# A graph layer on one core: table rows of two blocks and two relations by seven products of halves, weight sums on VectorE, and a table stage laid out by the list scheduler

## The chip, the cores and the metric

The kernel runs on one core of a Trainium2 chip. Its time is the device time of one execution in microseconds (us), from the records of the runs. TensorE (PE) multiplies matrices into PSUM, VectorE (DVE) and ScalarE (ACT) do elementwise work, GpSimd (POOL) does small elementwise work and issues the gathers from DRAM, and SyncE (SP) issues the plain transfers.

## The reference

One layer of a relational graph network on 625 nodes with 512 features. 20,625 edges (10,000 in both directions and one loop a node), sorted by target, have a source, a target, one of four relations and a weight. All is f32.

```python
h = maximum(layernorm(x), 0)
xs = h[src]
msg = sum over r of (xs @ W_rel[r] + b_rel[r]) * where(edge_type == r, edge_weight, 0)[:, None]
agg = segment_sum(msg, dst) / maximum(segment_sum(edge_weight, dst), 1)
t  = h @ W_self + b_self + agg
x1 = layer_norm(h + t, ln1_g, ln1_b)
ffn = gelu(x1 @ W_ffn1 + b_ffn1) @ W_ffn2 + b_ffn2
out = x + layer_norm(x1 + ffn, ln2_g, ln2_b)
```

W_rel is four matrices of 512 x 512, W_self one, W_ffn1 is 512 x 1024 and W_ffn2 1024 x 512.

## The kernel before

The nodes lie in five blocks of 125 rows (128 partitions are used). Two stages follow each other, and the second is in part begun inside the first.

**Table stage.** `h @ W_rel[r]` is worked out once for every node and relation. Each of the 20 pieces (`table_rows(r, i)`, relation r, block i) is one PSUM bank of 128 x 512 that four f32 matmuls fill, one for each 128 of the 512 inner features (the page counts two records for an f32 matmul, line L390). ScalarE empties the bank (L398), multiplying by the block's reciprocal standard deviation, for the normalization leaves that factor out: `pre_norm` (L352) only subtracts the mean and takes the maximum with zero. The row then goes to a DRAM table (L401); the last nine pieces are also kept in SBUF. The order is written out by hand: a double loop over r and i, with further work hung on chosen (r, i): the statistics and transposes of the next block, the search for the edges of each node (`find_tiles`, `rows_of_tiles`, `find_windows`, `slot_weights`, `slot_fields`), the degrees of nodes by relation, the loads of later weights (`later_loads`). Two buffers hold the four relation matrices in turn.

**Weights of the dense blocks.** For three blocks the edges are summed by matrices: for each target node, the sum of weights by (relation, source) makes a matrix `sums_w`, and the aggregate is `sums_w` times the table. It is built in 12 units (`slot_hots`: VectorE compares 16 slots with a grid and with keys, `low` L687, `eq` L690, and three products `high` L693; `slot_sums`: 16 small bf16 matmuls, L705; `empty_sums`: VectorE sums a bank, L711). Seven units (EARLY) are done inside the table stage, five behind it.

**Edge stage and rest.** The order comes from a list scheduler (`Plan`): operations have an engine, an assumed duration, dependencies and buffers that they take and give; its times settle only the order in which instructions are issued. In it: `h @ (W_self + I)` (pz, L428), the dense sums (`chunk_sum`, L1121), 82 gathers of table rows by GpSimd (L1000, L1054) that VectorE adds up seven edges at a time (L1024) for the other two blocks, with a one-hot matmul for each group (`edge_sum`; the sum is split into a high and a low part in a faster format, L1044 and L1045, apart from the last group, which is one f32 matmul, L1047), the first normalization (its root on GpSimd, L328), transposes (L335), the two layers of the feed-forward part (pu, L791, and po, L809), the second normalization and the store.

Of the kernel before, what the change touches and what calls it, by code (L numbers as in the profile page):

```python
# [68 lines left out]
class Plan:  # L69
# [6 lines left out]
    AFTER = {"PE": 1.5, "POOL": 0.8}  # L76

    def __init__(self, buffers):
        self.buffers, self.ops = dict(buffers), []

    def op(self, engine, us, fn, after=(), take=(), give=(), lag=0.08, rank=None, order=False, level=None):
        o = Plan.Op()
        o.engine, o.us, o.fn, o.take, o.give, o.lag, o.rank, o.level = engine, us, fn, list(take), list(give), lag, rank, level
        if engine == "PE":
            o.lag = max(lag, Plan.BEHIND)
        behind = Plan.AFTER.get(engine, 0.0)
        o.after = [(a, a.us if order and a.engine == engine else a.us + (0.0 if a.engine == engine == "PE" else a.lag)
                    + (behind if a.engine in ("DVE", "ACT") and a.engine != engine else 0.0)) for a in after if a is not None]
# [6 lines left out]
    def emit(self):  # L95
        for o in reversed(self.ops):
            o.tail = o.us + o.lag + max((b.tail for b in o.nexts), default=0.0)
        order = self.times()
        for o in order:
            if o.fn:  # L100
                o.fn()

    def times(self):
        left, order, t = list(self.ops), [], 0.0
        free, buffers, back = {"POOL": 3.0}, dict(self.buffers), []
# [33 lines left out]
def gnn_layer(ctx, tc, x, edges, edge_groups, firsts, fourths, windows, w_self, w_rel, w_ffn1, w_ffn2, brel_in, rows_in, bf1_in, out, n_edges):  # L139
# [38 lines left out]
    ps = ctx.enter_context(tc.tile_pool(name="ps", bufs=5, space=bass.MemoryType.PSUM))  # L178
    ps_acc = ctx.enter_context(tc.tile_pool(name="ps_acc", bufs=1, space=bass.MemoryType.PSUM))
    ps_add = ctx.enter_context(tc.tile_pool(name="ps_add", bufs=2, space=bass.MemoryType.PSUM))  # L180
# [3 lines left out]
    early = early_stack.enter_context(tc.tile_pool(name="early", bufs=1))  # L184

# [19 lines left out]
    def load_wr(r, ks=((0, KD),)):  # L205
        wr_sb.setdefault(r, None)
        if wr_sb[r] is None:
            wr_sb[r] = early.tile([P, KD, D], F32, tag="wr", name=f"wr_{r}", bufs=2)
# [18 lines left out]
    load_wr(0, [(2, 4)])  # L227
    nc.sync.dma_start(first_of_tile, bass.AP(tensor=firsts.tensor, offset=firsts.offset, ap=[[0, P], [1, NT]]))
    load_x(2, 3)
    load_x(3, NB)  # L230
    nc.sync.dma_start(ed, edges)
    load_wr(1)
# [4 lines left out]
    def later_loads(r, i):  # L237
        if (r, i) == (0, 0):
            bias_rows()
        if i == NB - 1 and r < R - 2:  # L240
            load_wr(r + 2)
        if (r, i) == (1, 2):
            nc.sync.dma_start(bf1, bf1_in)
            nc.sync.dma_start(ws_sb, w_self.rearrange("(k p) n -> p k n", p=P))
            load_rows(rows[:, :4 * D], 0, 4 * D)
            load_rows(rows[:, 5 * D:], 5 * D, 6 * D)
        if (r, i) == (2, 1):
            nc.sync.dma_start(w1_sb, w_ffn1.rearrange("(k p) f -> p k f", p=P))
        if r == 3 and i < LA:
            chunk_load(i * CH)  # L250
        if (r, i) == (2, 3):
            nc.sync.dma_start(w2_sb, w_ffn2.rearrange("(k p) n -> p k n", p=P))
# [27 lines left out]

    TB = 8
# [56 lines left out]
    def transposed(dest, in_, name):  # L338

        n = dest.shape[1]  # L340
        nc.scalar.copy(dest, turn(in_, name, n)[:, :n, :])
# [8 lines left out]
    def pre_norm(i, mean):  # L350
        if i > 0:
            nc.vector.tensor_scalar(z[:, i, :], xs[:, i, :], mean, 0.0, op0=ALU.subtract, op1=ALU.max)  # L352
# [1012 lines left out]
```

## Time and profile before

| | us |
|---|---|
| median of 3 runs (lowest to highest) | 245.45 (245.16 to 247.13) |
| the profiled execution | 246.03 |
| its span, first to last instruction | 244.0 |
| mean granted TensorE clock | 0.994 |

The span is the part of the execution that the trace shows; the remaining 2 us lie around it. In the tables of the profile, a row of a group has the line, engine, operation, tiles and shape, then "busy us, mean ns of one", then the idle time of that engine just before, with what ended it. A row of the timeline or of the chain has the start, the duration and the instruction. PEld is TensorE's loading of weights, which lies beside its matmuls.

### The profile page before, as it was taken

To read this page: it belongs to the slowest core of one execution; us is meant where nothing else is said; L and a number is where in the kernel's file an instruction comes from. 1 tells how busy PE (TensorE), PEld (TensorE's weight loads), DVE (VectorE), ACT (ScalarE), POOL (GpSimd) and SP (SyncE) were. 2 spreads that over 40 slices of the span, in tenths; PEclk is the share of its full clock that TensorE was granted. 3 is DMA by queue.
4 is the path that set the end of the run, shared out by engine and by line. 5 is a ranking of instruction groups with operands and counts; after the bars stand their busy time and mean duration, and the time that the engine had idled before them with its cause. 6 is when DMAs were issued, how large, how long until landed. Compare 5 with 4: busy or idle time off the path is not lost.

```text
span 244.0 us, 2881 instructions
## 1 busy us (share of the span) xinstructions
PE 235.2 (96%) x892; PEld 131.0 (54%) x892; DVE 190.6 (78%) x397; ACT 48.1 (20%) x87; POOL 119.1 (49%) x166
## 2 busy tenths in 40 slices
PE   7999999999999999999999999999999999999980
PEld 3454444555554555445554444457864588446860
DVE  5596399959699799999998989977987996473123
ACT  3233213212221211101020203012232042002500
POOL 6258505373100137877656788787877781110000
PEclk9999999999999999999999999999999999999997
DMA  6972586979986327677779898877966765001101
GB/s 162 357 262 61 173 267 197 371 240 358 284 275 179 125 54 210 181 205 208 198 208 334 271 305 322 297 234 247 351 201 191 210 181 163 0 1 42 45 3 46
DMA packets 20965, 48.91 MB, mean 200 GB/s; under 512 B 3162, under 2 KB 3924, under 8 KB 20818
## 3 DMA queue, kind: packets, MB, share of 16 engines
q1 hardware_dynamic: 13494, 26.11, 32.2%
q0 software_dynamic: 7152, 22.32, 30.8%
q10 hardware_dynamic: 300, 0.26, 0.4%
q8 instruction: 8, 0.13, 0.2%
q14 instruction: 11, 0.09, 0.1%
HBM read 42.27 MB, written 6.54 MB: 200 GB/s over the span
## 4 chain that ended last, share of the span: by engine, by line
PE 94%; DMA 2%; DVE 1%; SPq 1%; issue 0%
PE pt L390 28%; PE acc L1121 21%; PE po L809 14%; PE pu L791 14%; PE pz L428 7%; PE bank L705 5%; DMA wr<-in_L_gnn_W_rel_dram 2%; PE tp_x L335 1%; PE acc L1044 1%; PE acc L1045 1%; PE tp_h L335 1%; PE acc L1047 0%; PE tf L670 0%; DVE ya L828 0%; DVE y L833 0%
## 5 line engine op out<-in xcount | busy, mean ns | idle before, releaser
L1000 POOL DMA_INDIRECT ms<-table,row_i x70 | 69.8, 997 | 30.3 <-issue 12.6
L390 PE MATMUL pt<-wr,turned_x 128*128 128x512 f32 x160 | 72.1, 597 | 0.6 <-DMA wr<-in_L_gnn_W_rel_dram 0.6
L390 PEld LDWEIGHTS pt<-wr,turned_x 128*128 128x128 f32 x160 | 29.2, 190 | 32.3 <-issue 32.0
L1024 DVE SCALAR_TENSOR_TENSOR ea<-ms,wgt_g,ea 128x512 f32<-128x512 f32 x59 | 42.9, 746 | 1.3 <-DMA ms<-table,row_i 1.2
L809 PE MATMUL po<-w_sb,gelus 128*125 128x512 f32 (+2 forms) x96 | 35.5, 521 | 0.0
L791 PE MATMUL pu<-turned_x,w_sb 128*128 128x250 f32 (+1 forms) x192 | 35.3, 340 | 0.0
L791 PEld LDWEIGHTS pu<-turned_x,w_sb 128*128 128x128 f32 x192 | 31.4, 189 | 4.8 <-issue 1.9
L809 PEld LDWEIGHTS po<-w_sb,gelus 128*125 128x125 f32 x96 | 16.6, 188 | 15.3 <-issue 12.3
L398 ACT ACTIVATE m<-pt,rx 125x512 f32<-125x512 f32 x20 | 13.8, 688 | 53.4 <-PE pt L390 51.1
L711 DVE TENSOR_REDUCE sums_w<-bank 126x160 f32<-126x480 f32 x32 | 19.1, 650 | 6.2 <-PE bank L705 6.1
L705 PEld LDWEIGHTS <-low 128*128 128x128 bf16 x192 | 16.1, 147 | 13.1 <-issue 12.4
L1121 PE MATMUL acc<-tr,sums_w 126*128 126x512 f32 x44 | 20.6, 601 | 0.0
L428 PE MATMUL pz<-ws_sb,turned_x 128*128 128x512 f32 x40 | 17.8, 596 | 0.0
L1121 PE MATMUL acc<-m,sums_w 126*128 126x512 f32 x36 | 17.5, 603 | 0.0
L795 ACT ACTIVATE gelus<-pu,bf 128x250 f32<-128x250 f32 (+1 forms) x24 | 10.5, 437 | 31.5 <-PE pu L791 30.1
L705 PE MATMUL bank<-high,low 128*128 128x120 bf16 x192 | 16.2, 225 | 0.0
L693 DVE TENSOR_TENSOR high<-eq,turned 128x640 bf16<-128x640 bf16 x36 | 15.6, 487 | 0.4
L817 DVE TENSOR_TENSOR y<-po,z 125x512 f32<-125x512 f32 (+2 forms) x6 | 3.6, 602 | 14.3 <-PE po L809 14.3
L687 DVE TENSOR_TENSOR low<-turned,grid 128x2000 bf16<-128x2000 bf16 x12 | 14.3, 1192 | 0.1
L1054 POOL DMA_INDIRECT ms_first<-table,x_row x12 | 12.0, 997 | 3.5 <-issue 1.7
L1010 ACT CAST eh<-ea 128x512 fp32r<-128x512 f32 x9 | 5.3, 586 | 41.2 <-DVE ea L1024 41.2
L1121 PEld LDWEIGHTS acc<-tr,sums_w 126*128 126x128 f32 x44 | 7.9, 191 | 7.3 <-issue 6.9
(183 smaller groups left out, 241.8 us busy)
## 6 DMA issues: line engine op xcount, KB each, us to landing
tr<-table SPq DMA_DIRECT2D x10, 512.0 KB
table<-m SPq DMA_DIRECT2D x20, 224.0 KB
w_sb<-in_L_gnn_W_ffn_dram SPq DMA_DIRECT2D x2, 2048.0 KB
wr<-in_L_gnn_W_rel_dram SPq DMA_DIRECT2D x3, 1024.0 KB
xs<-in_x_dram SPq DMA_DIRECT2D x1, 1280.0 KB
ms<-table,row_i POOLq DMA_INDIRECT x70, 3.8
ws_sb<-in_L_gnn_W_self_dram SPq DMA_DIRECT2D x1, 1024.0 KB
rows<-in_rows_dram SPq DMA_DIRECT2D x1, 1024.0 KB
```

Source lines behind the costliest of these rows:

```text
L390: nc.tensor.matmul(p, hT[i][:, k, :], wr_sb[r][:, k, :], start=(k == 0), stop=(k == KD - 1))
L398: nc.scalar.activation(m[:NG], p[:NG], AF.Copy, scale=rx[:NG, i, 1:2])
L428: nc.tensor.matmul(p[0], hT[i][:, k, :], ws_sb[:, k, :], start=(k == 0), stop=(k == KD - 1))
L687: nc.vector.tensor_tensor(low[:, :, :NG, :], of[:, 0].rearrange("p (a t) -> p a t", t=TB).unsqueeze(2).to_broadcast([P, nb_, NG, TB]), gri ...
L693: nc.vector.tensor_mul(high[:, :, a * 2 * NC:(a + 1) * 2 * NC, :], eq, pairs(2 + a))
L705: nc.tensor.matmul(p[:, i * W:(i + 1) * W], low[:, t // TB, :, t % TB], high[:, t // TP, :, t % TP], start=True, stop=True)
L711: nc.vector.tensor_reduce(sums_w[OUTER[d]][:NG + 1, :, n0:n0 + 2 * QT].rearrange("p c (t h) -> p t h c", h=2), p[:NG + 1, :QT * 3 * 2 * NC ...
L791: nc.tensor.matmul(pu[:, :n_b * w], w1_sb[:, k, f * P:(f + 1) * P], turned_x[:, b0:b0 + n_b, k, :w], start=(k == 0), stop=(k == KD - 1))
L809: nc.tensor.matmul(po[h][:n, :w], gelus[:, at + i, f, :n], w2_sb[:, f, c], start=(f == 0), stop=(f == KF - 1))
L1000: nc.gpsimd.indirect_dma_start(out=ms[j], out_offset=None, in_=table[:, :], in_offset=bass.IndirectOffsetOnAxis(ap=row_i[:, j:j + 1], axis=0))
L1024: nc.vector.scalar_tensor_tensor(to, ms[j], wgt_g[:, k, q - 1:q], box["sum"], op0=ALU.mult, op1=ALU.add)
L1121: nc.tensor.matmul(acc[b,], sums_w[b][:NG + 1, c, :], kept[c][:NG + 1], start=done[b] == 1, stop=done[b] == NC)
```

## The change

**Seven products.** Blocks 1 and 2, and blocks 3 and 4, are taken in pairs (x, y); relations 0 and 1, and 2 and 3, in pairs (p, q). With the inner features in halves, a pair of blocks is a matrix of halves ((x0, x1), (y0, y1)) and a pair of relations ((p0, q0), (p1, q1)). Their product has eight half products; here it is formed from seven, with sums of the operands before and sums of results behind. Block 0 stays as it was (`plain`).

Four node sums a pair of blocks (128 x 2 x 128 elements each) and four weight sums a pair of relations (128 x 2 x 512 each) are made by VectorE. The weight sums of the second pair are written over the first pair's weights. Results are added up in PSUM: ScalarE copies a bank into the next one (`seeded`), and the following product is added to it there. Two of a unit's four rows are completed by VectorE, which adds a part that ScalarE has copied to SBUF (`row_of_two`); the other two, and block 0's, are emptied by ScalarE.

So that the sums can be formed, the normalization of blocks 1 to 4 now includes the factor (the root is needed ahead of it); for blocks 2 to 4 ScalarE does it, and the maximum with zero is in ScalarE's copy behind the transpose. Relations 2 and 3 have their weights loaded together, into the space of z and x, once all blocks are normalized and transposed; the first half of relation 1 comes ahead of block 3.

**The list scheduler** lays out the whole table stage. PSUM is five banks for products and three for the rest in this stage.

**Beside these:** five early units of slot weights in place of seven; the three products `high` of a unit are one instruction; several casts and scalings go from VectorE to ScalarE, the additions of the identity to W_self to GpSimd; the last edge group is split in two parts as the others are; some assumed durations of the second plan differ. Bank sums that the plan places behind the last product are issued in the edge stage.

```diff
-            wr_sb[r] = early.tile([P, KD, D], F32, tag="wr", name=f"wr_{r}", bufs=2)
+            wr_sb[r] = early.tile([P, KD, D], F32, name=f"wr_{r}") if r < 2 else (z, xs)[r - 2][:, :KD, :]
...
+        if i not in BY_ACT:
+            nc.vector.tensor_scalar(z[:, i, :], xs[:, i, :], mean, rx[:, i, 1:2], op0=ALU.subtract, op1=ALU.mult)
+        else:
+            nc.scalar.activation(z[:, i, :], xs[:, i, :], AF.Identity, scale=rx[:, i, 1:2], bias=rx[:, i, 2:3])
...
-    def table_rows(r, i, between=None):
...
-        nc.scalar.activation(m[:NG], p[:NG], AF.Copy, scale=rx[:NG, i, 1:2])
...
+    def row_of_two(c, p, m, e):
+        nc.vector.tensor_add(m[:NG], p[:NG], e[:NG])
...
+    def sums_of_nodes(x_, which):
+
+        S = node_sums[x_]
+        x0, x1, y0, y1 = (hT[b][:, h * HK:(h + 1) * HK, :] for b in (x_, x_ + 1) for h in range(2))
+        for n, (a, b, o) in enumerate(((y0, y1, ALU.add), (S[0], x0, ALU.subtract), (x0, y0, ALU.subtract), (x1, S[1], ALU.subtract))):
+            if n in which:
+                nc.vector.tensor_tensor(S[n], a, b, op=o)
+
+    def sums_of_weights(r, which):
+
+        T = weight_sums[r]
+        p0, p1, q0, q1 = (block_of_weights(r + n, h) for n in range(2) for h in range(2))
+        for n, (a, b) in enumerate(((q0, p0), (q1, T[0]), (q1, q0), (p1, T[1]))):
+            if n in which:
+                (nc.vector if T_ON[2 * r + n] else nc.gpsimd).tensor_tensor(T[n], a, b, op=ALU.subtract)
+
+    def product(to, of, with_, first):
+        for k in range(HK):
+            nc.tensor.matmul(to, of[:, k, :], with_[:, k, :], start=first and k == 0, stop=k == HK - 1, skip_group_check=True)
...
-        for a in range(3):
-            nc.vector.tensor_mul(high[:, :, a * 2 * NC:(a + 1) * 2 * NC, :], eq, pairs(2 + a))
-        return low, high
...
+        nc.vector.tensor_mul(high.rearrange("p n f k t -> p (n f) k t"),
+                             eq.unsqueeze(2).to_broadcast([P, np_, 3, 2 * NC, TP]).rearrange("p n f k t -> p n f (k t)"),
+                             w.rearrange("p n f t -> p (n f) t").unsqueeze(2).to_broadcast([P, 3 * np_, 2 * NC, TP]))
...
-    EARLY = 7
-    PER_ROW = 3
+    EARLY = 5
...
+                def seeded(k, of, o):
+                    return do("ACT", 0.57, lambda: nc.scalar.copy(at(k), at(of)), after=[o], take=["bank"])
+
+                o = pe(1.75, lambda: product(at("a"), x0, w(0), True), after=[turns[x_], weights if r else None], take=["bank"], read=["p0"])
+                b = seeded("b", "a", o)
+                yield
...
+                    o = pe(1.75, lambda: product(at("a"), x1, w(1), False), after=[b], read=["p1"])
+                    evicted(o, cx, names["a"], ["bank"])
...
+                o = pe(1.75, lambda: product(at("e"), node_sums[x_][0], weight_sums[r][0], True), after=[S[x_, 0], T[r, 0]], take=["bank"], read=["T0"])
+                e = do("ACT", 0.57, lambda: copied_e(names["e"]), after=[o], give=["bank"], take=["e"])
+                yield
+                o = pe(1.75, lambda: product(at("b"), node_sums[x_][1], weight_sums[r][1], False), after=[b, S[x_, 1], T[r, 1]], read=["T1"])
+                c = seeded("c", "b", o)
...
+                o = pe(1.75, lambda: product(at("b"), node_sums[x_][2], weight_sums[r][2], False), after=[c, S[x_, 2], T[r, 2]], read=["T2"])
+                d = seeded("d", "b", o)
+                f1 = evicted(o, cy + NB, names["b"], ["bank"], e=("sb_" + names["e"], e))
+                yield
+                o = pe(1.75, lambda: product(at("c"), node_sums[x_][3], w(3), False), after=[c, S[x_, 3]], read=["q1"])
+                f2 = evicted(o, cx + NB, names["c"], ["bank"], e=("sb_" + names["e"], e))
...
+                o = pe(1.75, lambda: product(at("d"), y1, weight_sums[r][3], False), after=[d, T[r, 3]], read=["T3"])
+                evicted(o, cy, names["d"], ["bank"])
...
+            here = plain(r)
+            for x_ in range(1, NB, 2):
+                there = unit(r, x_, r == 0 and x_ == 1)
+                for one in ("hhthttthtt" if r == 0 else "hhhthttttt") if x_ == 1 else "thttttt":
+                    next(here if one == "h" else there)
+                here = there
...
     def parted(unit):
-        return unit is not last_unit
+        return True
```

In the last lines "h" stands for a piece of block 0, or of the unit before, and "t" for a piece of the unit that is being formed, each of two matmuls.

More of the change, by code (lines that the diff above doesn't have):

```diff
@@ L378, in gnn_layer, with scaled_row, self_plus @@
     kept = {}
+    def scaled_row(g_bc):
+        nc.scalar.activation(g_bc, g_bc, AF.Copy, scale=1.0 / RS)
+    def self_plus():
+        for i in range(KD):
+            nc.gpsimd.tensor_add(ws_sb[:, i, i * P:(i + 1) * P], ws_sb[:, i, i * P:(i + 1) * P], ident)
     def bias_rows():
```

497 lines of the change are left out of this document (323 added, 174 removed).

## The prediction

> **What bounds the kernel now.** I read the page first (busy shares, then the chain that ended last), then the busy time by windows, then the chain of waits in order of time, and last the groups of single operations.
>
> ```profile
> PE 235.2 (96%) x892; PEld 131.0 (54%) x892; DVE 190.6 (78%) x397; ACT 48.1 (20%) x87; POOL 119.1 (49%) x166
> PE 94%; DMA 2%; DVE 1%; SPq 1%; issue 0%
> 0.00:85.80 85.80, 83.81 (x318) 41.61 (x319) 65.61 (x180) 20.23 (x34) 30.52 (x75) 1.00 0.73 235
> 85.80:161.70 75.90, 75.90 (x262) 37.17 (x260) 71.53 (x121) 9.68 (x16) 53.64 (x55) 1.00 0.75 236
> 161.70:210.50 48.80, 48.80 (x191) 34.70 (x190) 38.76 (x66) 12.90 (x25) 32.01 (x34) 1.00 0.67 205
> ```
>
> The window rows give length, then PE, PEld, DVE, ACT and POOL busy. The table stage runs from 0 to 85.8 us; behind it PE has no idle time at all up to 210.5. VectorE is 76% busy in the table stage (65.61 of 85.80), 94% in the first part of the edge stage (71.53 of 75.90), 79% after it. So TensorE is the bound, VectorE is close behind it, and the question is whether TensorE work that goes away is replaced by waiting for VectorE.
>
> **The products.** Twenty table rows of four f32 matmuls each were 80 matmuls. Now block 0 keeps four per relation (16), and each of four units (two blocks by two relations) has seven products of two matmuls (56): 72. Eight matmuls go, and each is two records (160 records for 80).
>
> ```profile
> L390 PE MATMUL pt<-wr,turned_x 128*128 128x512 f32 x160 | 72.1, 597 | 0.6 <-DMA wr<-in_L_gnn_W_rel_dram 0.6
> 20.89 18.89 PE pt L390 x44
> L705 PE MATMUL bank<-high,low 128*128 128x120 bf16 x192 | 16.2, 225 | 0.0
> 203.89 0.57 PE L1044 MATMUL acc<-eh,oh 128*128 128x512 f32 x1
> 204.31 0.39 PE L1045 MATMUL acc<-el,oh 128*128 128x512 f32 x1
> 204.54 3.54 PE L791 MATMUL pu<-turned_x,w_sb 128*128 128x250 f32 x16
> 209.63 1.02 PE L1047 MATMUL acc<-es,oh 128*128 128x512 f32 x2
> 210.48 8.75 PE L809 MATMUL po<-w_sb,gelus 128*125 128x512 f32 x20
> ```
>
> The mean of 597 ns holds overlap; the undisturbed stretch gives the step: 18.89/44 = 0.429 us a record. 16 x 0.429 = **6.9 us off PE**. The last group of edges is now split in a high and a low part as the others are: 0.65 us (203.89 to 204.54) in place of 0.85 (209.63 to 210.48), **0.2 us off PE**. Two of seven early units of slot weights move from the table stage behind it; that moves 32 of the 192 bank matmuls, 2.7 us, and saves nothing. Warm-up, transposes and bytes of weights are as many as before. With no new wait the profiled execution, 246.03 us for its span of 244.0, would become 246.03 - 7.1 = 238.9. The median of the runs shown, 245.45, lies 0.6 below that execution, so on its scale the floor is 238.3.
>
> **What VectorE is given.**
>
> ```profile
> L500 DVE TENSOR_TENSOR found<-ends,node_f 128x810 f32<-128x810 f32 x1 | 1.0, 1003 | 0.0
> L537 DVE TENSOR_TENSOR found<-ends,node_f 128x192 f32<-128x192 f32 x1 | 0.4, 357 | 0.0
> L817 DVE TENSOR_TENSOR y<-po,z 125x512 f32<-125x512 f32 x4 | 2.8, 691 | 5.2 <-PE po L809 5.2
> L687 DVE TENSOR_TENSOR low<-turned,grid 128x2000 bf16<-128x2000 bf16 x12 | 14.3, 1192 | 0.1
> L693 DVE TENSOR_TENSOR high<-eq,turned 128x640 bf16<-128x640 bf16 x36 | 15.6, 487 | 0.4
> L711 DVE TENSOR_REDUCE sums_w<-bank 126x160 f32<-126x480 f32 x32 | 19.1, 650 | 6.2 <-PE bank L705 6.1
> L352 DVE TENSOR_SCALAR z<-xs,mv_x 128x512 f32<-128x512 f32 x4 | 2.2, 543 | 0.1
> L952 DVE TENSOR_TENSOR ws_sb<-ws_sb,ident 128x128 f32<-128x128 f32 x4 | 1.1, 281 | 0.0
> L955 DVE TENSOR_SCALAR rows<-rows 128x512 f32<-128x512 f32 x2 | 0.8, 419 | 0.0
> L558 DVE CAST fields<-slot_f 128x384 bf16<-128x384 f32 x1 | 0.4, 424 | 0.0
> ```
>
> No sum of weights stands in the trace. Its size is 1024 f32 elements; the two "found" rows give (1003 - 357)/618 = 1.045 ns an element, so 1.23 us, and the bounds are 1.00 (the 810 row) and 2.0 (the 810 row taken twice). Eight are 9.8 us. Eight sums of nodes (256 elements) at 0.42 are 3.4. Eight rows are now finished by a VectorE addition from PSUM, 8 x 0.69 (the L817 row) = 5.5. Added: 18.7. Taken out: two early units, each 1.19 + 4 x 0.49 + 4 x 0.65 = 5.7, together 11.5 (moved, not saved); three normalizations, four additions on the self weights, two scalings (1.6 + 1.1 + 0.8) and nine casts, at most 0.42 each and mostly half as large, which I take as 2.5: 6.0, to ScalarE and GpSimd. The three multiplications of a unit become one of 1920 elements; the bf16 rows of 640 and 2000 elements give 0.49 + 1280 x 0.52 ns = 1.15 against 3 x 0.49, 0.3 a unit. If the new form loses the rate of those rows it costs 1920 x 1.045 ns = 2.0, 0.5 more a unit; I take the gain, since the operands have the same inner pairs as now.
>
> Table stage: 65.6 + 18.7 - 11.5 - 6.0 - 5 x 0.3 = 65.3 us of VectorE in 85.8 - 6.9 - 2.7 = 76.2 us, 86%. That is under the 94% at which PE has no idle time in the trace. Behind it: 71.5 + 38.8 + 11.5 - 7 x 0.3 + 0.7 (the extra low part) = 120.4 in 124.7 + 2.7 - 0.2 = 127.2 us, 95% in place of 88%. This is the tight place: if all of the moved work falls in the first part, that holds some 81 us in 78.6, so about 3 us must slide into the part that is 79% busy. I take 0.8 us of PE idle there, bounds 0 and 5.
>
> **The round trips.** In a unit ScalarE copies a partial sum from one PSUM bank to another and TensorE adds to the copy: twelve such seeds and four copies to SBUF.
>
> ```profile
> L341 ACT COPY turned_x<-tp_h 128x512 f32<-128x512 f32 x4 | 2.3, 586 | 7.1 <-PE tp_h L335 7.1
> 9.07 1.92 PE L390 MATMUL pt<-wr,turned_x 128*128 128x512 f32 x4
> 11.10 0.69 ACT L398 ACTIVATE m<-pt,rx 125x512 f32<-125x512 f32 x1 [1.24 <-PE pt L390]
> ```
>
> ScalarE starts 0.1 us after the modelled end of its matmuls (9.07 + 1.92 = 10.99, then 11.10). So a seed takes 0.1 + 0.59 + about as much back, near 0.8 us. In the order of the pieces each seed has one other product between it and its use, four records, 1.7 us. It is covered with 0.9 us to spare; if that cover goes, it costs 0.8 each. ScalarE, 20.2 us busy in 85.8, gets 16 copies (9.4), three normalizations and the casts and gives eight evictions back: under half full. A seed queued behind another ScalarE copy can still be late now and then: 0.5 us in all, bounds 0 and 10 (twelve times 0.8). The node and weight sums are VectorE's, and PE, in order, holds every later product and slot sum behind one that waits for them; a row finished by VectorE holds one of the five banks that the next unit needs. Within the 86% I leave that in the same 0.5.
>
> **The first microseconds.** The load order changes (first half of relation 1 ahead of block 3), and normalizing now needs the reciprocal root from GpSimd first.
>
> ```profile
> 7.70 1.10 PE L390 MATMUL pt<-wr,turned_x 128*128 128x512 f32 x2 [0.59 <-DMA wr<-in_L_gnn_W_rel_dram]
> 10.41 0.69 DVE L369 BATCH_NORM_STATS2 st_x<-xs 128x6 f32<-128x512 f32 x1 [1.98 <-DMA xs<-in_x_dram]
> 142.22 0.75 DVE L1024 SCALAR_TENSOR_TENSOR ea<-ms,wgt_g,ea 128x512 f32<-128x512 f32 x1
> 142.49 0.60 POOL L328 TENSOR_TENSOR rs_z<-rs_z,half 128x1 f32<-128x1 f32 x1
> 149.32 0.74 DVE L752 SCALAR_TENSOR_TENSOR za<-z,mv_z,rows 128x512 f32<-128x512 f32 x1
> 149.58 0.89 POOL L328 TENSOR_TENSOR rs_z<-rs_z,half 128x1 f32<-128x1 f32 x1
> ```
>
> Block 2 lands at 10.41. Statistics 0.69, three small VectorE steps (an estimate of 0.5), root 0.6, normalization 0.69, transposes 0.44, ScalarE's copy 0.59, node sum 0.42, and eight hand-overs at an estimated 0.2 end near 15.9. PE, from 7.70, has 0.86 of the first product left, four half rows at 1.72 and two sets of transposes until it wants that sum: 16.3. So 0.4 us in hand, and any delay lands on PE: 0.8 us, bounds 0 and 3. The weights of relations 2 and 3 are now loaded together into the space of x and z; they are wanted after some nineteen pieces, past 40 us, and I charge nothing, or up to 2 us if that cover goes.
>
> Beside VectorE work that reads one SBUF operand (142.22) the root takes 0.60 us; beside work that reads two (149.32) it takes 0.89. The sums of weights read two and are longer. [...]
>
> **Is the gather chain a floor?**
>
> ```profile
> 89.25 1.15 POOL L1000 DMA_INDIRECT ms<-table,row_i  x1 [6.63 <-PE pz L428]
> 200.71 1.51 POOL L1000 DMA_INDIRECT ms<-table,row_i  x1 [0.30 <-issue]
> 204.74 0.75 DVE L1024 SCALAR_TENSOR_TENSOR es<-ms,wgt_g,ea 128x512 f32<-128x512 f32 x1
> 219.07 0.60 PE L335 MATMUL tp_x<-ident,x 128*128 128x128 f32 x4
> ```
>
> GpSimd gathers table rows from 89.25, 3.4 us behind the table, to 202.2; the last row is added at 205.5. The matmul of that group waits in PE's order until 209.63, and the last transposes until 219.07: 13.6 us behind the last row, for about 6 us of dependent work. So some 7 us of room, and the chain itself starts up to 9.6 us earlier. Even if VectorE stretches it by 5, it does not end last.
>
> **Sum.** 246.03 - 6.9 - 0.2 + 0.8 + 0.5 + 0.8 = 241.0; on the scale of the median **240.4 us**.
>
> **The rivals.** *The full root-and-sum collision* at the start: GpSimd's root held for the length of a weight sum (1.2 us) in blocks 1 and 2, 2.4 us in place of part of my 0.8: 242.5. For it: the 0.89 us row and only 0.4 us in hand. Against: at that time most weights for the sums have not landed. Chance 0.08. *VectorE becomes the bound* in the edge stage: at no more than 94% its 81 us need 86 where PE needs 78.6, and half of that difference is made good later: 4 us, 244.5 (243 to 247). For it: 94% already. Against: room after 161.7 and in the table stage. Chance 0.15. *Seeds on the path*, the slower case: ScalarE's copy, in ScalarE's queue behind evictions and field copies, comes after PE has run out of the one covering product. Each then costs 0.8 plus a queued eviction's 0.69, 1.5 x 12 = 18 in all less the cover that remains, a third: 12 us, so 250.3. It decides against the change from 7.1/12 = 0.6 us a seed. For it: every product of a unit hangs on another engine, where the trace has none such. Against: ScalarE's free time. Chance 0.11. *No effect*, PE idle exactly where products went, 245.5: chance 0.02.
>
> **How the numbers follow.** The forecast has 0.64, by itself 238.2 to 242.3. One per cent (about what a measurement tells from no change) is 243.0 and 247.9. Faster: 0.64 + 0.06 + 0.02 (the low end of VectorE's bound) = 0.72; within: 0.02 + 0.11 + 0.02 = 0.15; slower: 0.11 + 0.02 = 0.13. The range 238.2 to 245.8 leaves out the seeds (0.11), the top of VectorE's bound (0.04) and 0.05 below.
>
> **What would show it.** Right: 144 table records with steps of 0.43, table stage over near 77 to 79, PE idle of 2 to 3 us more than before. Wrong: PE waiting on ScalarE copies inside units (seeds), on node sums before 20 us (root), or gaps in PE between 85 and 160 that end on slot weights (VectorE); and weight sums well over 1.3 us, or the merged product near 2.

## The result: 3242 us, because the plan lets a product overwrite marks that are still to be counted

| | median, us | lowest to highest | runs | span of the profiled execution |
|---|---|---|---|---|
| before | 245.46 | 245.16 to 247.13 | 4 | 244.0 |
| after | 3242.11 | 3240.62 to 3245.42 | 4 | 3243.2 |

The ratio is 13.18 with a 95% interval of 13.14 to 13.22. The forecast was 240.4, its range 238.2 to 245.8. Runs e1 to e4 and e9 to e16 fell on chips on which the kernel before itself took 259 to 263 us and the traces have gaps of up to 5.2 us that no wait of the kernel explains. Ratios are not steady there either: one and the same kernel came out at 1.042 (e15) and, on another chip, at 1.001 (e17). So of those runs only three things are read: whether the loop ran, the order of instructions, and single times and waits outside the gaps; their ratios are given, and a difference of one or two per cent between them settles nothing. The other runs fell where before took 245.5 to 245.7. A ratio leaves out the executions that are over 1.5% above the fastest of their kernel, so it can differ from the quotient of the medians beside it.

The page of the changed kernel, its head, the line of the granted clock and two of its groups:

```profile
span 3243.2 us, 23738 instructions
PE 1732.4 (53%) x4596; PEld 919.8 (28%) x4596; DVE 1164.3 (36%) x2679; ACT 90.2 (3%) x176; POOL 440.7 (14%) x499
PEclk9996766776677667766776677667766776677777
L1507 PE MATMUL pg<-gm,gelus 128*125 128x512 f32 x1620 | 1334.8, 924 | 1391.0 <-DVE gm L1499 1391.0
L1489 POOL DMA_INDIRECT gm<-table,gi x162 | 153.3, 947 | 2412.5 <-DVE gw L1500 2412.5
```

The count of instructions says it before any time does: 23738, where before had 2881, and 4596 records on TensorE where eight matmuls should have gone from 892. The new lines are not of the change. Both kernels end in a branch: the fast form (dense sums, gathers, first edges) counts the edges that it does not cover (`n_out`, from `cnt` and `x_missing`), and if that count is above zero a general loop adds up all edges again, one tile of 128 edges in each of 162 turns, and then does the five blocks once more. Before, the loop is not entered. After, the layer ends as it should, near 245 us, and then the loop runs. The timeline of the changed kernel's TensorE, first matmuls of two turns (start, duration, instruction, and in brackets the idle time before and its releaser):

```profile
253.93 2.04 PE L1507 MATMUL pg<-gm,gelus 128*125 128x512 f32 x2 [12.97 <-DVE gm L1499]
271.18 2.04 PE L1507 MATMUL pg<-gm,gelus 128*125 128x512 f32 x2 [8.71 <-DVE gm L1499]
```

The last turn starts its matmuls at 3001.55, so a turn takes (3001.55 - 253.93)/161 = 17.07 us and 162 take 2765. With 245 for the layer that leaves some 233 for the blocks done again. In each turn TensorE waits 8 to 9 us (1391.0 in all, 8.6 a turn) for two gathers and the addition of what they bring.

Why is the count above zero? The first edges of the sparse blocks have marks `x_on`, 1 where the edge belongs to the node. GpSimd multiplies them (`first_weights`); VectorE sums them into `x_found` and takes that from `x_missing` (`first_counted`); GpSimd then overwrites `x_on` with the shares, weight times reciprocal degree (`first_shares`). The timeline around these in the kernel before:

```profile
82.07 0.17 DVE L644 TENSOR_REDUCE x_found<-x_on 128x1 f32<-128x12 f32 x1 [0.32 <-POOL x_on L642]
...
82.27 0.16 DVE L645 TENSOR_TENSOR x_missing<-x_missing,x_found 128x1 f32<-128x1 f32 x1
...
82.41 0.21 POOL L646 TENSOR_TENSOR x_on<-x_step,rdeg 128x12 f32<-128x12 f32 x1
```

and in the changed kernel:

```profile
69.56 0.21 POOL L709 TENSOR_TENSOR x_on<-x_step,rdeg 128x12 f32<-128x12 f32 x1
...
70.03 0.15 DVE L705 TENSOR_REDUCE x_found<-x_on 128x1 f32<-128x12 f32 x1
...
70.21 0.16 DVE L706 TENSOR_TENSOR x_missing<-x_missing,x_found 128x1 f32<-128x1 f32 x1
```

The two have changed places. Their pieces in the plan are

```python
piece("counted", "DVE", 0.33, first_counted, "first", "groups", "counts")
piece("shares", "POOL", 0.45, first_shares, "first", "degrees")
```

"counted" waits for `groups` and `counts` on a full VectorE; "shares" is not told to come after it. The scheduler issues it first, the sum runs behind it (from 70.03, where the shares end at 69.77), and so it is a sum of shares, each below 1. `x_missing` stays above zero.

### The profile page after: what moved, and what is told of

The parts are those of the page before. It is cut to its first block, busy times and chain, and to the rows that moved or that the text cites. A ratio compares the mean times of both kernels' runs of the same rounds, so it can differ in the third digit from the quotient of the medians.

```text
span 3243.2 us, 23738 instructions
## 1 busy us (share of the span) xinstructions
PE 1732.4 (53%) x4596; PEld 919.8 (28%) x4596; DVE 1164.3 (36%) x2679; ACT 90.2 (3%) x176; POOL 440.7 (14%) x499
## 5 line engine op out<-in xcount | busy, mean ns | idle before, releaser
L1507 PE MATMUL pg<-gm,gelus 128*125 128x512 f32 x1620 | 1334.8, 924 | 1391.0 <-DVE gm L1499 1391.0
L1508 DVE TENSOR_TENSOR z<-z,pg 125x512 f32<-125x512 f32 x810 | 557.1, 688 | 944.0 <-PE pg L1507 944.0
L1507 PEld LDWEIGHTS pg<-gm,gelus 128*125 128x125 f32 x1620 | 352.8, 270 | 1400.2 <-issue 1400.2
L1509 PEld LDWEIGHTS pd<-ones,gelus 128*125 128x125 f32 x1620 | 424.9, 262 | 657.3 <-issue 657.3
L1489 POOL DMA_INDIRECT gm<-table,gi x162 | 153.3, 947 | 2412.5 <-DVE gw L1500 2412.5
L1499 DVE TENSOR_TENSOR gm<-gm,gb 128x512 f32<-128x512 f32 x162 | 112.1, 692 | 702.6 <-DMA gb<-table,gt 702.6
L1509 PE MATMUL pd<-ones,gelus 128*125 128x1 f32 x1620 | 273.6, 238 | 0.0
L1496 POOL DMA_INDIRECT gb<-table,gt x162 | 153.1, 945 | 49.4 <-issue 49.4
L1502 DVE TENSOR_SCALAR gelus<-node_row,gw 128x640 f32<-128x640 f32 x162 | 99.2, 612 | 5.9
L863 PE MATMUL pu_again<-turned_x,w_sb 128*128 128x128 f32 x320 | 47.8, 324 | 3.4 <-ACT turned_x L342 3.4
```

The source lines that it names most:

```text
L863: nc.tensor.matmul(pu[:, :n_b * w], w1_sb[:, k, f * P:(f + 1) * P], turned_x[:, b0:b0 + n_b, k, :w], start=(k == 0), stop=(k == KD - 1))
L1489: nc.gpsimd.indirect_dma_start(out=gm, out_offset=None, in_=table[:, :], in_offset=bass.IndirectOffsetOnAxis(ap=gi[:, 0:1], axis=0))
L1496: nc.gpsimd.indirect_dma_start(out=gb, out_offset=None, in_=table[:, :], in_offset=bass.IndirectOffsetOnAxis(ap=gt[:, 0:1], axis=0))
L1499: nc.vector.tensor_add(gm, gm, gb)
L1502: nc.vector.tensor_scalar(go, node_row, gw[:, 0:1], gw[:, 1:2], op0=ALU.is_equal, op1=ALU.mult)
L1507: nc.tensor.matmul(pg[:NG], go[:, b * NG:(b + 1) * NG], gm, start=True, stop=True)
```

## The experiments

### What makes the loop run

Theory 1 is the order above; the rival was that a cast which moved to ScalarE rounds a value that VectorE did not, so that the count itself changes.

**e1**, the dependence that is missing:

```diff
-        piece("shares", "POOL", 0.45, first_shares, "first", "degrees")
+        piece("shares", "POOL", 0.45, first_shares, "first", "degrees", "counted")
```

> The changed kernel with one dependency more: the multiplication of x_on by the inverse degrees (shares, GpSimd) is planned behind the count of x_on (counted, VectorE). Theory 1 (the plan lets the multiplication overwrite x_on before it is summed, so the count of edges outside comes out above zero and the general loop behind the layer runs): the loop is not entered, and the time is what the changed kernel's trace shows up to the last store, 248 to 250.5 us. Theory 2 (casts of integers on ScalarE give other values and so another count): the loop still runs, 3,240 us. If the prediction's sum held apart from that loop: 240 to 242 us.

Measured 264.51 where before took 262.84 on that chip, ratio 1.002 (0.996 to 1.008): the loop is gone. The 248 to 250.5 can't be held against a chip like this one; e5 repeats the run.

**e2**, the kernel before with the same fault, its multiplication moved ahead of the sum:

```diff
+        nc.gpsimd.tensor_mul(x_on, x_step[:, :, 1:, 0], rdeg...)
         nc.vector.reduce_sum(x_found, x_on...)
         nc.vector.tensor_sub(x_missing, x_missing, x_found)
-        nc.gpsimd.tensor_mul(x_on, x_step[:, :, 1:, 0], rdeg...)
```

> The kernel before, with its multiplication of x_on by the inverse degrees moved ahead of the sum of x_on, and nothing else. Theory 1: the general loop runs, 3,230 to 3,250 us. Theory 2: no integer cast is on ScalarE here, so 245 to 247 us.

Measured 3255.1 in one run, with 23734 instructions. One line moved ahead of two others brings the whole effect to the old kernel.

**e3**, the changed kernel with its casts back on VectorE, and the order left:

```diff
-            piece(f"ends{n}", "ACT", 0.3, lambda a=a, e=e: nc.scalar.copy(ends_w[:, a:e], win[:, a:e, 1, :]), f"rows{n}")
+            piece(f"ends{n}", "DVE", 0.3, lambda a=a, e=e: nc.vector.tensor_copy(ends_w[:, a:e], win[:, a:e, 1, :]), f"rows{n}")
...
```

> The changed kernel with the casts that it moved to ScalarE put back on VectorE, the count left as the plan orders it. Theory 1: the general loop still runs, about 3,240 us. Theory 2: 246 to 252 us.

Measured 3263.68 in one run; its trace still has the shares at 74.9 and the sum of the marks behind them, at 83.8. The rival falls.

**e9**, the changed kernel with every instruction in its place, and the shares in a tile of their own:

```diff
+    x_share = const.tile([P, INNER, EG - 1], F32, name="x_share")
...
-        nc.gpsimd.tensor_mul(x_on, x_step...
+        nc.gpsimd.tensor_mul(x_share, x_step...
...
```

> The changed kernel in its own order, every instruction where it stands, but the weighted shares of the first edges go to a tile of their own (128 x 12) and no longer over the marks that VectorE still has to count. Theory 1 (the marks were overwritten, the kernel counted edges as missing and went through the general loop): the loop's 162 turns of about 17 us are gone, 248 to 251 us, since in the changed kernel's own trace the last group of po stands 3.8 us later than before (233.88 to 240.95, against an end of 237.15), so 245.5 + 3.8 = 249.3, and what follows it may cost up to 1.5 more. Rival (something else enters the loop as well): above 3200.

Measured 265.51 beside 258.95 for before, ratio 1.027 (1.016 to 1.038). No loop; the 248 to 251 were meant for a chip at 245.5, and 1.027 times that is 252, a little above them. e9 keeps the order (shares ahead of the sum) and takes away only the overwriting, so the overwriting that this order allows is the cause of the 3242.

### What the repaired kernel takes

**e4 to e8** ask why the repair still is not faster. **e5** is e1 again, and **e4** and **e6** are it with the two units back in the table stage:

```diff
-    EARLY = 5
+    EARLY = 7
```

> As the first run, with seven units of slot weights in the table stage as before in place of five. Theory A (behind the table VectorE has too much to do, so that it frees the gathers' buffers late, and the gather chain ends last): two units, some 11 us of VectorE, leave the edge stage; the gather chain takes 4 to 10 us less and the time falls to 242 to 247 us. Theory B (waits of TensorE inside the table stage took the gain): the table stage is fuller, so no better or 1 to 4 us slower, 249 to 254 us.

> The kernel of the first run once more, since on the chip of that run the kernel before itself took 257 to 267 us at a lower clock. By the first 244 us of the changed kernel's trace: 248 to 250.5 us, 1 to 2% above the kernel before. By the prediction's sum apart from the loop: 240 to 242 us.

> As e4, on another chip. Theory A (VectorE, with more to do behind the table, frees the gathers' buffers late, and the gather chain ends last): 243 to 247.5 us, the gather chain 4 to 10 us shorter than in the run beside it. Theory B (TensorE's waits inside the table stage took the gain): 249 to 254 us.

e4: ratio 1.001 (0.991 to 1.011), which settles nothing. e5: 249.33 (247.85 to 252.34) beside 245.69, ratio 1.013 (1.006 to 1.019), inside its 248 to 250.5. e6: 253.43, ratio 1.029 (1.025 to 1.034), inside theory B's range. The units are no better off in the table stage: TensorE waits there 1.8 us at 78 and 2.5 us at 81 for VectorE's `low`.

e5 is what the forecast can be held against. Its busy time by stage (length, then PE, PEld, DVE, ACT and POOL busy, the granted clock, the share of the DMA engines, GB/s):

```profile
0.00:82.10 82.10, 75.99 (x271) 36.13 (x271) 66.40 (x161) 29.51 (x64) 38.95 (x79) 1.00 0.73 249
82.10:239.19 157.09, 154.23 (x606) 91.19 (x606) 131.42 (x213) 26.73 (x51) 92.92 (x91) 1.00 0.58 179
239.19:246.90 7.71, 0.00 (x0) 0.00 (x0) 2.94 (x10) 0.29 (x1) 0.00 (x0) 0.74 0.13 36
```

| us | before | forecast | e5 | e5 less forecast |
|---|---|---|---|---|
| table stage | 85.8 | 77.5 | 82.1 | +4.6 |
| from there to the last po | 151.35 | 154.65 | 157.09 | +2.4 |
| tail | 6.85 | 6.85 | 7.71 | +0.9 |
| span | 244.0 | 239.0 | 246.9 | +7.9 |

And e5's waits of TensorE (engine, line, what it waited for: us in total, times, longest):

```profile
PE d L448 <- ACT d L1080: 1.7, 1, 1.7
PE acc L1280 <- ACT eh L1246: 1.4, 1, 1.4
PE pt L1121 <- DMA wr<-in_L_gnn_W_rel_dram: 1.2, 2, 1.0
PE bank L777 <- DVE sums_w L783: 1.2, 2, 0.9
...
PE tp_x L336 <- DVE x L828: 0.7, 1, 0.7
PE tp_h L336 <- DVE z L375: 0.6, 1, 0.6
PE acc L1281 <- DVE el L1250: 0.5, 2, 0.3
```

Before, this list had 0.8 us beside the warm-up. The largest entry is one seed. The timeline of e5 at it:

```profile
39.37 0.35 ACT L1152 CAST ends<-win 128x192 f32<-128x192 int32 x1 [2.95 <-DMA win<-in_windows_dram,at_i]
...
40.33 0.57 ACT L1080 COPY d<-b 128x512 f32<-128x512 f32 x1
...
40.96 1.55 PE L448 MATMUL d<-w_sb,turned_x 128*128 128x512 f32 x3 [1.74 <-ACT d L1080]
```

ScalarE, in order, stood 2.95 us at a cast of the windows, whose transfer had not landed, and the seed d stood behind it. The plan takes the windows to land 2.3 us after their issue; the median of these transfers in e5 is 7.1 us, and 4.0 in the kernel before.

**e7** has the planned stage with 80 plain products: no sums, no seeds, rows emptied by ScalarE.

```diff
-                o = pe(1.75, lambda: product(at("e"), node_sums[x_][0], weight_sums[r][0], True), ...
...
+                        def part(c=c, b=b, q=q, h=h):
+                            p = row(c, b, r + q)
+                            for k in range(h * HK, (h + 1) * HK):
+                                nc.tensor.matmul(p, hT[b][:, k, :], wr_sb[r + q][:, k, :], start=(k == 0), stop=(k == KD - 1))
```

> The repaired kernel with plain products in the same planned layout: 80 matmuls of the table in place of 72, no sums of nodes and of weights, no copies between banks, all 20 rows emptied by ScalarE. TensorE gets 6.9 us more, VectorE 18 us less. If TensorE's work sets the end: 253 to 257 us. If VectorE and the gather chain set it (theory A): within 2 us of the run beside it or faster, 245 to 250 us.

Measured 259.35, ratio 1.050 (1.043 to 1.058), 10 us above e5 and above both ranges. The planner orders everything anew here, so that 10 is not a clean price of the products: the wait of ScalarE for the windows is larger in it, and TensorE loses 3.6 us behind it. Its timeline:

```profile
51.91 0.30 ACT L1124 CAST ends<-win 128x128 f32<-128x128 int32 x1 [7.15 <-DMA win<-in_windows_dram,at_i]
...
53.67 0.56 PE L777 MATMUL bank<-high,low 128*128 128x120 bf16 x4 [3.62 <-DVE sums_w L783]
```

**e8** gives the making of slot weights a later level in the second plan, so that gathered rows are added first.

```diff
-rank=(0.55, i), level=0.18 if d < 2 else S_LEVEL)
+rank=(0.55, i), level=0.25)
```

> The repaired kernel with one number changed in the second plan: VectorE's slot weights (levels 0.18) come after the additions of gathered rows (level 0.2) where both could go. Theory A: the gathers wait less for buffers, the chain is 3 to 8 us shorter, but dense sums wait longer for their weights; 245 to 249 us. Theory B: the gathers' buffers don't matter, and TensorE waits more: 250 to 254 us.

Measured 262.64, ratio 1.061 (1.051 to 1.070), above the ranges of both theories: TensorE now waits 6.5 us in one piece for VectorE's `high`. VectorE itself had stood 5.3 us at a gathered row that had not landed and that now came ahead of the weights in its order.

### Taking the sums away

**e10** and **e11** keep the order of e9 and leave instructions out; the products then read plain halves.

```diff
-                    T[r, n] = do("DVE", 1.18, lambda r=r, n=n: sums_of_weights(r, (n,)), ...
+                    T[r, n] = do("DVE", 1.18, None, ...
...
```

> As the run with shares in a tile of their own, in the same planned order, but the eight sums of weights are left out and the products take plain halves of the weights, so what comes out is not the layer's. VectorE has 8 x 1.22 = 9.8 us less in the table stage and nothing else moves. Theory V (VectorE's amount of work gives the gain back): the table stage ends up to 3 us sooner and the VectorE work that spills into the edge stage is gone: 243 to 247, at least 3 us below the run with all sums. Theory L (the order itself: seeds behind queued copies, gathers, groups of edges): within 1.5 us of the run with all sums, 248 to 251.

> As the run without weight sums, and the eight sums of nodes (0.42 us each) are left out too, so VectorE has 13.2 us less, in the same planned order; what comes out is not the layer's. Theory V: 241 to 245, one or two us below the run without weight sums alone, since the first product that waits on a node sum at 17 us (0.9 us) goes too. Theory L: 247 to 250.

Beside e9's 265.51 (ratio 1.027) they took 262.77 (1.014, 1.004 to 1.024) and 263.52 (1.020, 1.011 to 1.029). The table stage ended at 79.89 and 80.37 instead of 81.74. The three intervals overlap, so the medians alone don't tell the runs apart; in the traces 9.8 us of VectorE are worth 1.85 us of table stage (2.7 by the medians, between the two theories), and 3.4 more are worth nothing that can be seen. The wait for the seed is there without any sum (1.0 and 1.4 us), as is 0.8 us at the stage's end.

**e12** has half of the weight sums on GpSimd.

```diff
-    T_ON = (1, 1, 1, 1, 1, 1, 1, 1)
+    T_ON = (1, 1, 1, 1, 0, 0, 0, 0)
...
-                    T[r, n] = do("DVE", 1.18, ...
+                    T[r, n] = do("POOL", 1.6, ...
```

> The repaired kernel (shares after the count, 249.3) with the four weight sums of relations 2 and 3 on GpSimd in place of VectorE, so that half of the change's weight sums on VectorE is undone; the planner orders everything anew. VectorE has 4.9 us less. Theory V: 245 to 248. Rival (GpSimd's long sums and VectorE's instructions hold each other, and the searches and gathers on GpSimd come later): 250 or more.

Measured 265.70, ratio 1.025 (1.015 to 1.036). That is on the rival's side, as e9 on the same chip is without the edit (1.027): taking 4.9 us from VectorE in this way gains nothing. One VectorE comparison is long beside two of the sums; which of the rival's reasons costs the time is not shown. That comparison and two of the four sums in its timeline:

```profile
45.73 5.16 DVE L592 TENSOR_TENSOR found<-ends,node_f 128x128 f32<-128x128 f32 x1
...
46.06 2.36 POOL L444 TENSOR_TENSOR wr<-xs 128x1024 f32<-128x1024 f32 x1
...
59.53 3.26 POOL L444 TENSOR_TENSOR wr<-xs,wr 128x1024 f32<-128x1024 f32 x1
```

On GpSimd the sum takes 2.36 to 3.26 us for VectorE's 1.22, and the plan had it at 1.6. The comparison takes 5.16 us on 128 x 128 elements; at 39.89, with no sum beside it, one on 128 x 192 takes 0.36.

### Mending the two waits, and moving two units by hand

**e13** sets the landing time of the windows, **e14** makes the last group whole again, **e16** does both and puts three assumed times of the second plan back. **e15** is the kernel before with five early units.

```diff
-            piece(f"rows{n}", "POOL", 1.3 * (e - a), ..., lag=2.3)
+            piece(f"rows{n}", "POOL", 1.3 * (e - a), ..., lag=6.5)
...
-        return True
+        return unit is not last_unit
...
-    GATHER = 1.25
+    GATHER = 1.3
-    SLACK = 1.0
-    LATER = 0.2
+    SLACK = 1.2
+    LATER = 0.3
```

```diff
-    EARLY = 7
+    EARLY = 5
```

> The repaired kernel with one assumed time of the planner changed: the windows' transfers are taken to land 6.5 us after their issue in place of 2.3, so that the casts that wait for them are placed later in ScalarE's queue and the seed d of the first unit stands ahead of them. Theory S (that seed is on the path: TensorE waited 1.74 us for it at 40.96): the wait is gone and the time is 1.0 to 1.7 us under the repaired kernel, about 1.006 of before. Rival (the table stage then ends on VectorE's bank sums instead, or the new order costs more elsewhere): 1.010 of before or more.

> The repaired kernel with the last group of edges again as one f32 matmul in place of a high and a low part. Prediction: the split takes 0.2 us off TensorE, so undoing it gives +0.2. Theory G (the chain of gathers now ends last, and the split puts a cast on ScalarE and a subtraction on VectorE behind the last row; TensorE waited 1.36 and 0.22 us there): 0.8 to 1.4 us under the repaired kernel, about 1.008 of before.

> The kernel before with one edit: five early units of slot weights in place of seven, so that 11.5 us of VectorE work and 32 small matmuls move from the table stage behind it, as the change does. No products of sums, no planned table stage. The prediction's term: TensorE's amount is the same, VectorE in the edge stage goes to some 95% and that costs 0.8 us: 246.3, ratio 1.003. Theory G (in the edge stage VectorE's adding of gathered rows falls behind, the buffers come free late, the gathers end some 9 us later and the last blocks wait for them): 248 or more, ratio at least 1.010.

> The repaired kernel with the later landing time for the windows, the last group whole, and the three assumed times of the second plan (a gather, its slack, a later one) as they were before. If the two waits (1.74 at the seed, 1.58 at the last group) are what is left on the path: 249.3 - 3.3 = 246.0, ratio 1.002. To beat the kernel before it would have to save more than that, which the theories do not give. If VectorE's amount fills each gap anew: 1.010 or more.

Measured, each beside 260.58 for before: 1.042 (1.028 to 1.056), 1.033 (1.007 to 1.059), 1.042 (1.026 to 1.058), 1.012 (1.004 to 1.020). What can be read of these is the waits, not the times (e15 has gaps of 5.07 and 3.02 us that the same kernel lacks in e17, below): in e13 the seed's wait is 0.3 us, where e14 on the same chip has 1.6, and a wait of 3.3 on bank sums has come at 79, as it has in e16.

**e17** and **e18** repeat e15 and e16.

> The kernel before with five early units in place of seven, again, on another chip. The prediction's term (0.8 us for VectorE at 95% in the edge stage): ratio 1.003. Theory G (gathers held by VectorE's adding): ratio 1.010 to 1.030, the gathers' idle time behind VectorE's ea well over that of the kernel before, and TensorE waiting in the edge stage on bank sums or rows.

> The repaired kernel with the later landing time, the last group whole and the three assumed times as before, again, on another chip. If the waits at the seed and at the last group were the path: ratio 1.000 to 1.004. If VectorE's amount fills each gap anew: 1.010 to 1.016. Below 0.995 it would beat the kernel before, which no theory here gives.

e17: 246.20 (245.90 to 246.76) beside 245.69, ratio 1.001 (0.998 to 1.003). Theory G is right that the gathers end later (below), and its price falls: TensorE waits for none of it, and moving two units costs at most a few tenths of a per cent by itself, as the prediction had it. e18: 249.21 (249.04 to 249.63), ratio 1.014 (1.011 to 1.017). The wait at the last group is gone from it and the one at the seed is 0.3 us, and yet it takes as long as e5, as the second theory had it.

What took their place is a wait for VectorE, which is full in the second half of the table stage. Busy times from 46 us to the end of that stage, in the kernel before, in e17 and in e5:

```profile
46.00:85.80 39.80, 39.80 (x199) 21.64 (x198) 33.03 (x68) 8.10 (x13) 7.85 (x25) 1.00 0.78 248
```

```profile
46.00:83.80 37.80, 37.80 (x168) 19.64 (x166) 24.64 (x53) 7.51 (x13) 7.58 (x25) 1.00 0.79 263
```

```profile
46.00:82.10 36.10, 34.88 (x163) 18.12 (x161) 35.07 (x68) 13.04 (x31) 15.11 (x38) 1.00 0.74 252
```

VectorE (the third pair) is 83% busy there before, 65% in e17 and 97% in e5. Ahead of 46 us it is busy for 31.33 us in e5, and the longest of its waits there is at the first weight sum of relations 2 and 3, whose weights had not landed:

```profile
39.16 1.22 DVE L444 TENSOR_TENSOR wr<-xs,z 128x1024 f32<-128x1024 f32 x1 [6.64 <-DMA xs<-in_L_gnn_W_rel_dram]
```

No run here tries an earlier load, or other work put ahead of that sum. In e18 the wait comes at the end of the stage; its windows and its TensorE at that place:

```profile
77.90:81.20 3.30, 0.01 (x1) 0.00 (x0) 3.25 (x6) 0.54 (x2) 0.00 (x0) 0.80 0.50 161
81.20:86.00 4.80, 4.79 (x31) 3.77 (x32) 4.08 (x8) 0.00 (x0) 2.76 (x3) 0.50 0.27 69
86.00:93.00 7.00, 7.00 (x27) 3.34 (x26) 6.31 (x8) 0.69 (x1) 5.78 (x5) 0.95 0.57 156
```

```profile
81.21 3.02 PE L777 MATMUL bank<-high,low 128*128 128x120 bf16 x28 [3.30 <-DVE sums_w L783]
84.02 8.43 PE L475 MATMUL pz<-ws_sb,turned_x 128*128 128x512 f32 x16
```

For 3.3 us TensorE has nothing to do while VectorE is busy for 3.25. And the price is higher than the wait: the granted clock (the number behind the five pairs) is 0.50 for at least the 4.8 us that follow, and pz takes 8.43 us, where e5's takes 7.13.

The other half is the chain of gathers. First gather and last added row in e5, and in e17:

```profile
83.25 1.07 POOL L1236 DMA_INDIRECT ms<-table,row_i  x1 [11.30 <-DVE sums_w L783]
...
213.41 0.75 DVE L1260 SCALAR_TENSOR_TENSOR ea<-ms,wgt_g,ea 128x512 f32<-128x512 f32 x1 [1.88 <-DMA ms<-table,row_i]
```

```profile
88.11 1.46 POOL L1000 DMA_INDIRECT ms<-table,row_i  x1 [9.37 <-issue]
...
213.60 0.75 DVE L1024 SCALAR_TENSOR_TENSOR es<-ms,wgt_g,ea 128x512 f32<-128x512 f32 x1
```

Before, this took from 89.25 to 205.49, 116.2 us. In e17 it takes 126.2 and ends at 214.35, and TensorE comes to the last group at 216.40, after it, so nothing waits. In e5 it starts 6 us earlier than before, takes 130.9, ends at 214.16, and TensorE is there first and waits 1.36 and 0.22.

No run here beats the kernel before.

## Why the prediction was wrong

**The step that failed** is in "The products": "With no new wait the profiled execution, 246.03 us for its span of 244.0, would become 246.03 - 7.1 = 238.9." It takes for granted that the new order runs the same program. A table stage that had been in a hand-written order was given to a scheduler which knows only the dependences it is told, and one that the hand-written order kept without saying so, a tile read before it is overwritten, was lost. A count that steers a branch came out wrong, and the branch cost 2765 us for its turns and some 233 behind them. e1, e2, e3 and e9 show this from four sides. None of the rivals was of this kind; all asked what would be late, and none what would be overwritten early.

**With the fault mended** the kernel takes 249.33, still above the range. In the profiled executions e5 is 7.9 us above the forecast. TensorE's work fell by 5.0 us in all where 7.1 was forecast (2.1 of the 7.9), its idle time rose from 2.0 to 9.0 where 2.1 more was charged (4.9), and the tail grew by 0.9. This is where:

"The products". A step was 0.43 us as forecast: in e5's timeline four records take 1.72 from start to start.

```profile
28.75 1.88 PE L448 MATMUL d<-w_sb,turned_x 128*128 128x512 f32 x4
30.47 1.88 PE L448 MATMUL e<-w_sb,z 128*128 128x512 f32 x4
32.19 1.88 PE L448 MATMUL b<-w_sb,z 128*128 128x512 f32 x4
```

The sums and seeds came out at their prices. Groups of e5 (busy us, mean ns of one):

```profile
L763 DVE TENSOR_TENSOR high<-eq,turned_w 128x1920 bf16<-128x1920 bf16 x12 | 13.9, 1158 | 0.5
L420 DVE TENSOR_TENSOR m<-c,sb_e 125x512 f32<-125x512 f32 x4 | 2.7, 686 | 0.0
L444 DVE TENSOR_TENSOR w_sb<-wr,w_sb 128x1024 f32<-128x1024 f32 x2 | 2.4, 1217 | 0.0
...
L1080 ACT COPY d<-b 128x512 f32<-128x512 f32 x4 | 2.3, 575 | 3.4 <-PE b L448 2.0 <-DVE m L420 1.5
...
L436 DVE TENSOR_TENSOR first_S<-turned_x 128x256 f32<-128x256 f32 x2 | 0.8, 418 | 0.0
```

1.16, 0.69, 1.22, 0.58 and 0.42 us, against 1.15, 0.69, 1.23, 0.59 and 0.42. But TensorE's work in the table stage fell by 83.83 - 75.99 = 7.8, not by 9.6. By start-to-start times without the waits, the products fell from 69.6 to 63.8, 5.8 for 6.9, as pieces behind bank matmuls or behind a wait take longer (in the changed kernel's trace 1.77 at 57.77 and 1.82 at 40.80, for 1.72), and the bank matmuls by 1.5 for 2.7, as I had taken their busy time, which overlaps their neighbours (before, eight at 80.56 are busy for 0.66 and the next product starts 0.50 behind their start).

"What VectorE is given". The amount was right (66.40 us for 65.3, which is 81% of the longer stage for 86%), and the share was wrong as a bound: until 46 us VectorE waits, for loads above all, and the rest of the stage holds 97%. The term was put behind the stage, where I feared 95%; there e17 shows no wait for VectorE and only one of 0.7 us, for a ScalarE copy at 223, so the 0.8 was enough. The rival "VectorE becomes the bound" comes nearest to what happened, but it stood at the wrong place, and its price of 4 us left out the halved clock behind a long wait, which e6 (0.56 on the mean of 83.16 to 86, behind 2.48) and e18 (0.50 behind 3.30) show and e5 (1.00) escaped. Of all this e10 gives 1.85 us of table stage to the weight sums.

"The round trips". Twelve seeds cost 1.74 us in e5 where 0.5 was charged. That lies inside the bounds of 0 and 10 by luck, for it came not by the road named (evictions ahead of a seed) but by one cast that waited for a transfer. e13 and e18 take that wait to 0.3, and e18 is no faster for it.

"The first microseconds". TensorE's waits before 20 us beside the warm-up rose from 0.8 to 2.0, by 1.2 where 0.8 was charged and 3 was the bound. The first product of a node sum, forecast for 16.3, starts at 17.47 and waits 0.13 for it; the rest stands at loads and transposes. Of the prediction's estimates for the way to it, the three small VectorE steps are 0.18, 0.15 and 0.21 us in the changed kernel's trace (9.58 to 10.82), near the 0.5; the hand-overs there are 0.03 to 0.09 us, and the 0.2 charged for each does not show. That the weights of relations 2 and 3 are wanted past 40 us held for TensorE's products, and not for VectorE's sums, which stood 6.64 us for them. In the changed kernel a root fell under a weight sum:

```profile
21.42 1.21 DVE L444 TENSOR_TENSOR w_sb<-wr,w_sb 128x1024 f32<-128x1024 f32 x1
21.46 1.58 POOL L329 TENSOR_TENSOR rx<-rx,half 128x1 f32<-128x1 f32 x1 [0.66 <-DVE rx L381]
```

The root takes 1.58 us, 1.0 more than the 0.60 of a root beside work that reads one operand, near the whole of the 1.21 of the sum that it meets. TensorE did not wait for that root.

"Is the gather chain a floor?" "Even if VectorE stretches it by 5, it does not end last." It was stretched by 14.7; e17, whose only change is the two moved units, has 10 of them. Together with the split of the last group, which puts a cast and a subtraction behind the last row, it ends last by 1.6 us. The 0.2 that the split was to save does not show: in e5 its two matmuls run from 214.89 to 215.96, which is 0.85 without the 0.22 of waiting between them, as long as the one f32 matmul (216.40 to 217.25 in e17). The 1.6 of waiting came on top. With the last group whole (e18) the stretch from the first pz to the start of the last group of po is 148.96 for e5's 150.02, although the first 2.7 us of e18's pz run at half the clock.

Two things stay open. One is how much of the 249 is the load of VectorE and how much the chain of gathers: the edits that eased one let the planner reorder the other. The other is the tail's 0.9 us, which lies behind VectorE's last instruction, at the last store.

## What to carry to other kernels

When a hand-written order is given to a scheduler, list for every tile that is written twice who reads the first value, and give the second write that reader as a dependence; give it a tile of its own where that costs only a few bytes. After a change, compare the number of instructions before any time: 23738 for 2881 tells of a branch, whatever the busy shares say. And read how full an engine is from the stretch in which its work can lie, not from the stage: 81% of the stage was 97% of the part that counted.

## What was not expected of the hardware

A wait of TensorE can cost nearly twice its length. In e18, 3.3 us without work were followed by 5.5 at a granted clock of 0.50 (81.2 to 86.7), which by estimate is 2.7 us lost behind the 3.3; in e8, behind 6.5 us at 144, it was at 0.50 until 164, with two more waits in between; after e5's 1.74 at 39 the clock stayed at 1.00. The stretches at 0.50 last 3.41 us (e13, from 83.5), 6.83 (e18, from 79.9), 10.24 (the changed kernel in its loop, from 266.9) or 17.07 (e8, from 147.2), all multiples of 3.41. In the windows of e1, e4, e6, e8 to e14, e16 and e18, every gap of 2.2 us or over had a stretch at 0.50 behind it, lone gaps under 1.5 us (1.21 at 48.0 in e16, 1.41 at 38.5 in e11) had none, and between them both occur (1.53 us at 164 in e10 did, 1.74 at 39 in e5 and 2.16 at 131 in e16 did not). Before, no such wait existed (the longest beside the warm-up is 0.6 us), and so the prediction's charge of a wait at its own length had nothing in the trace to correct it.
